# Two fp4 stages of a macaron block: the normalisation plan of group 2 is moved, and the last 64 features of the down product become two rounded-float32 products

## The chip, the cores and the metric

The kernel runs on one core of one Trainium2 chip. The metric is the device time in microseconds of one launch, weights' preparation included. A core has five engines with a queue each, worked in order: PE (matrix products), DVE (vector), ACT (activations), POOL (a second, slower vector engine) and SP (which issues transfers). They meet through semaphores only.

## The reference, cut to what matters

Six residual steps are applied to x of shape (8, 1024, 256). The first and the third are the fp4 feed-forward that the change touches:

```
def fp4_quant_dequant(x):                 # blocks of 16 along the last axis
    scale = max(max(abs(xb)) / 6, 1e-12)
    q = GRID[searchsorted(MID, abs(xb / scale))] * sign(xb) * scale
def fp4_linear(x, w):
    return einsum('bsk,nk->bsn', fp4_quant_dequant(x), fp4_quant_dequant(w))
h = silu(fp4_linear(x, w_gate)) * fp4_linear(x, w_up)      # 704 features
return fp4_linear(h, w_down)                               # back to 256
x = x + 0.5 * ffn(layernorm(x))
```

The others are a decayed linear attention, a ternary feed-forward (twice) and an attention with memories. Results are compared in float32.

## The kernel before, in words

x stays on the chip: 16 groups of 4 tiles, a tile being 128 tokens by 256. The stages follow one another: fp4, decay attention, fp4, ternary, memory attention, ternary. The function `ffn_fp4` is called twice, first with `prepare` set (it then also rounds and turns the down weights, and prepares later stages' weights).

One step i of its loop works on several tiles at once. PE multiplies tile i by gate and up in two halves of 352 (lines 835: `pg`, then `pu`), turns the scales of tile i-1 (line 863, once per step), and multiplies tile i-4 by the down weights: six 128x128 by 128x256 float32 products (line 932), the last of which holds 64 real features and 64 zeros. ACT applies silu to `pg` (line 846), DVE multiplies it by `pu` (line 848). DVE finds the block maxima of h (783 to 787), POOL divides by them (791), ACT makes the magnitudes (795) and in the next step DVE rounds in two passes (858), the second writing the grid values in bfloat16 to `gd`. SP turns `gd` by a transposing DMA into `gt` (884) and spreads the turned scales to a wide tile `ht` through DRAM (871, 876). Two steps later POOL multiplies `ht` by `gt` (899), and the step after it the tile goes into line 932. DVE adds the result to x (941).

Beside that, x of a coming group is normalised by ACT (317, 325, two tiles at a time) into the one buffer `xn`, divided by its scales (line 791 with `xn`), rounded in place by DVE (`mgx`, 858) and turned by a second transposing DMA, `gtx<-xn` (line 1048), which POOL multiplies with scales (899 with `xt`). For a group t this lies in steps 4t-7 (normalise tiles 0, 1), 4t-6 (scale), 4t-5 (normalise tiles 2, 3; round half 0), 4t-4 (scale half 1; DMA of half 0), 4t-3 (round half 1; POOL's product of half 0). The statistics come from a plan (`PLANS`, `statistics`, `advance`): sizes of batches and the step at which each is due; the shares of a batch are spread over the steps before it, and those due at step 0 (`first`) are worked off in the stage before by `begin`.

Every instruction of these stages is pinned behind the one pinned before it on its engine (`pin`), so the order in the queue is the order in the text; within a step of the loop: products with silu, copies of scales and magnitudes, `spread`, the DMA `gtx`, `advance`, normalising, POOL's products (`scaled_turn`), `scale` of h, x's scale and rounding, the down products. The last two tiles are turned on PE by `turn` (line 920) and not by DMA.

Of the kernel before, what the change touches and what calls it, by code (L numbers as in the profile page):

```python
# [9 lines left out]
F32 = mybir.dt.float32  # L10
F32R = mybir.dt.float32r
# [7 lines left out]
P = 128  # L19
D = 256  # L20
# [19 lines left out]
def macaron_kernel(  # L40
# [227 lines left out]
    def statistics(sizes, dues):  # L268
# [78 lines left out]
        "start": ((2, 1, 1, 2, 4, 4, 2), [max(0, G * (g - 2) + 1) for g in range(NG)]),  # L347
        "fp4": ((2, 1, 1, 2, 4, 4, 2), [max(0, G * (g - 2) + 1) for g in range(NG)]),
# [95 lines left out]
    wd = w_f0.tile([P, NC, D], F32, name="wd")  # L444
    nc.gpsimd.memset(wd[DCH[-1][1] :, NC - 1, :], 0.0)
# [190 lines left out]
    def prep_down_turn(ps, tag):  # L636
        for i, (k0, kn) in enumerate(DCH):
            pt = ps.tile([P, D], F32, tag=tag, name="ptd")
            for c in range(2):
                pin(  # L640
                    nc.tensor.transpose(
                        pt[:kn, c * P : (c + 1) * P], wd_n[:, c, k0 : k0 + kn], ident
                    )
                )
            pin(nc.scalar.copy(wd[:kn, i, :], pt[:kn, :]))
# [99 lines left out]
    def ffn_fp4(prepare, after):  # L745
        with ExitStack() as st:
# [13 lines left out]
            nc.gpsimd.memset(gd[:, NI:], 0.0)  # L760
# [18 lines left out]
            def scale(v, pool, at, mul=nc.gpsimd, sc=None):  # L779
# [10 lines left out]
                copies.append(lambda: pin(nc.scalar.copy(sc, sp)))  # L790
# [75 lines left out]
            def spread(i, pt):  # L866
# [19 lines left out]

                turn_grid()
# [16 lines left out]

            def scaled_turn(i):
                hs.pop(i)
                ht = spreading.pop(i)
                multiplied(ht, turning.pop(i))
                hts[i] = (ht, P)

            def turn(i):
                h, _ = hs.pop(i)
                ht = hp.tile([P, NC, P], F32, tag="ht", name="ht", bufs=HT_BUFS)
                for c0, c1 in ((0, 4), (4, 5), (5, 6)):
                    kn = DCH[c0][1]
                    pa = ps_t.tile([P, 4, P], F32, tag="pt", name="pt")
                    for c in range(c0, c1):
                        k0 = DCH[c][0]
                        pin(
                            nc.tensor.transpose(pa[:kn, c - c0, :], h[:, k0 : k0 + kn], ident)  # L920
                        )
                    pin(nc.scalar.copy(ht[:kn, c0:c1, :], pa[:kn, : c1 - c0, :]))
                hts[i] = (ht, DCH[-1][1])

            def down(i, ps=ps_o, tag="po"):
                g, j = divmod(i, G)
                ht, tail = hts.pop(i)
                po = ps.tile([P, D], F32, tag=tag, name="po")
                for c in range(NC):
                    kn = tail if c == NC - 1 else P  # L930
                    pin(
                        nc.tensor.matmul(  # L932
                            po,
                            lhsT=ht[:kn, c, :],
                            rhs=wd[:kn, c, :],
                            start=(c == 0),
                            stop=(c == NC - 1),
# [49 lines left out]

            xn = None
# [5 lines left out]
            for i in range(NT + 3):  # L994
                g, j = divmod(i, G)
                h = hp.tile([P, NI], F32, tag="h", name="h") if i < NT else None

                to = (i + 7) // G
                to_do = to < NG and i > 0
                half = 0 if j in (1, 2, 3) else 1  # L1000
# [43 lines left out]
                for to_, half_ in list(xgrids):  # L1044
                    gx, at = xgrids[to_, half_]
                    if at == i - 1:
                        gt = lnp.tile([P, G, P], BF16, tag="gtx", name="gtx", bufs=1)
                        pin(nc.sync.dma_start_transpose(out=gt, in_=gx))
                        xgrids[to_, half_] = (gt, at)
# [7 lines left out]
                if to_do and j % 2 == 1:  # L1057
                    if j == 1:
                        to_n, tiles = to, (0, 1)
                        if xn is None:  # L1060
                            xn = xn_pool.tile([P, G, D], F32, tag="xn", name="xn")
                    else:
                        to_n, tiles = (i + 5) // G, (2, 3)
                    if to_n < NG:
                        for n in tiles:
                            ln.normalize(xn, to_n, n, pin)
                if by_dma(i - 3):
                    scaled_turn(i - 3)
                if NT - 2 <= i - 2 < NT:
                    turn(i - 2)  # L1070
                for key in list(xgrids):
                    gt, at = xgrids[key]
                    if at == i - 2:
                        xgrids.pop(key)
                        to_m, half_m = key
                        multiplied(xts[to_m][:, G * half_m : G * half_m + G, :], gt)
                if i < NT:
                    own = scales[i % 2] if by_dma(i) else None
                    if own is not None:
                        scale(h, hp, NI, sc=own[:, : NI // 16])  # L1080
# [4 lines left out]
                    if j % 2 == 0 and i > 1:  # L1085
                        to_s, half_s = ((i + 6) // G, 0) if j == 2 else ((i + 4) // G, 1)
                        if 1 < to_s < NG:
                            scale(
                                x_part(half_s), lnp, NI + 88,
                                sc=own[:, NC * 8 : NC * 8 + 2 * D // 16],  # L1090
                            )
                            xhalf[i] = (to_s, half_s)
                    if j % 2 == 1 and i > 1:
                        to_r, half_r = ((i + 5) // G, 0) if j == 3 else ((i + 3) // G, 1)
                        if 1 < to_r < NG:
                            v = x_part(half_r)
# [988 lines left out]
```

## Time and profile before

| | us |
|---|---|
| three runs | 2606.8, 2608.18, 2610.64 |
| median | 2608.18 |
| the profiled execution | 2604.35 |
| its span in the profile | 2602.6 |
| fp4 stage 1, first gate product to last down product | 35 to 563 |
| fp4 stage 2, the same | 1006 to 1503 |
| busy over the span: PE, DVE, ACT, POOL | 2504, 2108, 1236, 903 |

The profile is one execution. Its parts used here are busy time by engine, busy shares in 40 slices, groups of instructions (busy time, mean of one, idle time before), the chain of work that ended last, and the timeline of instructions with the idle time before each and what ended it. L932 means line 932 of the kernel before.

### The profile page before, as it was taken

The page shows a single profiled execution, that of the slowest core. Times are in us where ns is not written, and L with a number is a line of the kernel's source. Part 1 is how long each engine was busy: PE and PEld are TensorE (multiplying, and loading weights), DVE is VectorE, ACT ScalarE, POOL GpSimd, SP SyncE. Part 2 cuts the span into 40 slices and gives each one's busy share as a digit, 9 for nine tenths or more (in the row PEclk, how much of TensorE's full clock was granted, in tenths as well). Part 3 has the DMA queues.
Part 4 walks back from the last instruction along what each step waited for, and adds up shares of the span by engine and source line. Part 5 has one row for each costly group of instructions (what it writes and reads, how often), then busy time and mean ns, then how long its engine had stood idle before and what let it go on. Part 6 is the DMA issues. An engine that isn't in the chain of part 4 may idle for free.

```text
span 2602.6 us, 52695 instructions
## 1 busy us (share of the span) xinstructions
PE 2504.2 (96%) x20426; PEld 1864.2 (72%) x20426; DVE 2107.9 (81%) x5040; ACT 1235.8 (47%) x2785; POOL 902.6 (35%) x895
## 2 busy tenths in 40 slices
PE   4899999999999998999999999999999999999999
PEld 2566776766666665677777789995677767678998
DVE  7899999858777678998889789657888888879864
ACT  5344444433433333444444366665555555437664
POOL 4555555521100102555555400004555555540000
PEclk9899999999999999999999999999999999999999
DMA  7455565510000001556555300000000000000001
GB/s 218 99 111 120 119 114 112 110 32 2 2 2 2 2 2 29 113 117 116 115 114 118 81 1 1 1 1 1 2 2 2 2 2 2 2 2 25 33 33 42
DMA packets 197883, 130.32 MB, mean 50 GB/s; under 512 B 137824, under 2 KB 173696, under 8 KB 197632
## 3 DMA queue, kind: packets, MB, share of 16 engines
q1 hardware_dynamic: 196688, 125.75, 22.3%
q8 instruction: 161, 2.64, 0.4%
q0 software_dynamic: 240, 0.54, 0.1%
q14 instruction: 90, 0.74, 0.1%
q10 hardware_dynamic: 704, 0.66, 0.1%
HBM read 78.67 MB, written 16.52 MB: 37 GB/s over the span
## 4 chain that ended last, share of the span: by engine, by line
PE 80%; DVE 11%; ACT 3%; DMA 3%; issue 2%; POOL 1%; SPq 1%; DVEq 0%; POOLq 0%; ACTq 0%
PE po L932 10%; PE po L1207 9%; PE pg L835 9%; PE ph L1180 9%; PE pu L835 8%; PE sc L1250 5%; PE py L1334 5%; PE pq L1348 4%; PE pkv L1348 4%; PE pk L1348 4%; PE po L1348 4%; PE py L1316 2%; PE pmo L1765 2%; DVE at L1259 1%; DMA gtx<-xn 1%
## 5 line engine op out<-in xcount | busy, mean ns | idle before, releaser
L835 PE MATMUL pg<-wgu,xt 128*128 128x352 f32 x1024 | 350.0, 465 | 13.4 <-ACT sg L846 13.1
L932 PE MATMUL po<-wd,ht 128*128 128x256 f32 x1536 | 356.0, 382 | 2.3 <-DVE x L941 1.8
L835 PE MATMUL pu<-wgu,xt 128*128 128x352 f32 x1024 | 348.9, 464 | 2.1 <-DVE h L848 1.9
L932 PEld LDWEIGHTS po<-wd,ht 128*128 128x128 f32 x1536 | 291.7, 191 | 66.0 <-issue 4.1
L791 POOL TENSOR_TENSOR h<-h,q_rs 128x704 f32<-128x704 f32 (+1 forms) x128 | 176.3, 1378 | 419.9 <-DVE q_rs L787 419.9
L846 ACT ACTIVATE sg<-pg 128x352 f32<-128x352 f32 x256 | 117.8, 460 | 399.3 <-PE pg L835 394.0
L835 PEld LDWEIGHTS pg<-wgu,xt 128*128 128x128 f32 x1024 | 194.9, 192 | 108.5 <-ACT sg L846 21.1
L835 PEld LDWEIGHTS pu<-wgu,xt 128*128 128x128 f32 x1024 | 187.1, 193 | 103.3 <-issue 14.7
L1207 PE MATMUL po<-w,hl 128*128 128x256 f32 x1024 | 243.9, 280 | 1.4 <-DVE hl L1191 1.2
L1207 PE MATMUL po<-w,hh 128*128 128x256 f32 x1024 | 243.4, 280 | 0.0
L1881 POOL TENSOR_TENSOR mo<-mo 128x256 f32<-128x256 f32 x192 | 164.3, 856 | 195.0 <-DVE mo L1778 186.5
L899 POOL TENSOR_TENSOR ht<-gt,ht 128x768 f32<-128x768 bf16 x124 | 206.4, 1664 | 0.0
L1180 PE MATMUL ph<-xh,w 128*128 128x512 f32 x512 | 204.4, 401 | 1.4 <-ACT hf L1188 0.6
L1180 PE MATMUL ph<-xl,w 128*128 128x512 f32 x512 | 202.2, 396 | 0.0
L1191 DVE TENSOR_TENSOR hl<-hf,hh 128x512 fp32r<-128x512 f32 x256 | 168.2, 683 | 39.6 <-ACT hh L1189 36.1
L1207 PEld LDWEIGHTS po<-w,hl 128*128 128x128 f32 x1024 | 192.1, 188 | 4.5 <-DVE hl L1191 2.5
L1207 PEld LDWEIGHTS po<-w,hh 128*128 128x128 f32 x1024 | 192.0, 188 | 2.6 <-DVE x L1215 0.3
L848 DVE TENSOR_TENSOR h<-sg,pu 128x352 f32<-128x352 f32 x256 | 131.6, 514 | 60.0 <-PE pu L835 53.1
L1188 ACT ACTIVATE hf<-ph,b1c 128x512 f32<-128x512 f32 x256 | 168.3, 696 | 18.5 <-PE ph L1180 16.1
L1259 DVE TENSOR_TENSOR at<-sc,dec 128x512 f32<-128x512 f32 x256 | 158.5, 681 | 16.6 <-PE sc L1250 16.5
L1259 DVE TENSOR_TENSOR at<-sc,tri 128x512 f32<-128x512 f32 x256 | 164.6, 678 | 0.4 <-PE sc L1250 0.4
L1189 ACT CAST hh<-hf 128x512 fp32r<-128x512 f32 x256 | 149.2, 628 | 17.0 <-PE po L1207 15.2
(276 smaller groups left out, 5304.0 us busy)
## 6 DMA issues: line engine op xcount, KB each, us to landing
ht<-sd SPq DMA_DIRECT2D x124, 384.0 KB
xt<-sd SPq DMA_DIRECT2D x56, 256.0 KB
sd<-sct SPq DMA_DIRECT2D x124, 64.0 KB
x<-in_x SPq DMA_DIRECT2D x15, 512.0 KB
out<-x SPq DMA_DIRECT2D x15, 512.0 KB
raw_w<-in_w_t SPq DMA_DIRECT2D x2, 1024.0 KB
gt<-gd SPq DMA_TRANSPOSE x124
gtx<-xn SPq DMA_TRANSPOSE x56
```

Source lines behind the costliest of these rows:

```text
L791: pin(mul.tensor_tensor(vb, vb, rs[:, :, None].to_broadcast([P, nb, 16]), ALU.mult))
L835: nc.tensor.matmul(ps, lhsT=xts[g][:, 2 * j + k, :], rhs=wgu[:, k, (2 * q + of_up) * NHALF : (2 * q + of_up + 1) * NHALF], start=(k == 0), ...
L899: nc.gpsimd.tensor_tensor(wide.rearrange("p c t -> p (c t)"), grid.rearrange("p c t -> p (c t)"), wide.rearrange("p c t -> p (c t)"), ALU. ...
L932: nc.tensor.matmul(po, lhsT=ht[:kn, c, :], rhs=wd[:kn, c, :], start=(c == 0), stop=(c == NC - 1),)
L1180: nc.tensor.matmul(ph, lhsT=w1[:, k, f * P : (f + 1) * P], rhs=xt[:, k, :], start=(k == 0 and xt is xh), stop=(k == 1 and xt is xl),)
L1188: nc.scalar.activation(hf, ph, AF.Gelu, bias=b1c[:, f : f + 1])
L1189: nc.scalar.copy(hh[:, f, :], hf)
L1191: nc.vector.tensor_tensor(hl[:, f, :], hf, hh[:, f, :].bitcast(F32), ALU.subtract)
L1207: nc.tensor.matmul(po, lhsT=ht[:, f, j * P : (j + 1) * P], rhs=w2[:, f, :], start=(f == 0 and ht is hh), stop=(f == NF - 1 and ht is hl),)
L1259: nc.vector.tensor_tensor(at, sc.rearrange("p m (e t) -> p (m e) t", e=2), weight, ALU.mult)
L1348: nc.tensor.matmul(dst, lhsT=lhsT, rhs=rhs, start=n == 0, stop=n == len(parts) - 1)
L1881: summed = nc.gpsimd.tensor_tensor(mo[:, :, :, 0, :], mo[:, :, :, 0, :], mo[:, :, :, m, :], ALU.add)
```

## The change

- The plan of stage 1 has group 2's statistics due one step later; in stage 2 the first batch is three groups, so that group 2's statistics are done ahead of the stage. In both stages group 2 is normalised in step 2 (tiles 0, 1; it was step 1) and step 3 (tiles 2, 3, as before), scaled in 3 and 4 (2 and 4), rounded in 4 and 5 (3 and 5). Later groups keep their steps.
- Within a step, POOL's products (`scaled_turn` and x's) now stand ahead of the issue of the DMA `gtx`, which stands ahead of normalising.
- The last 64 features are kept twice: ACT copies the last 64 columns of `gd` into the columns after them, and the last four scales likewise. The wide product of the last chunk thus holds them in 128 rows. `split` makes its rounded float32 `hh` (ACT) and the rest `hl` (POOL). The weights `ws` hold the rounded weights in 64 rows and the rest in the other 64. The sixth float32 product becomes `hh` by `ws` and `hl` by `ws`.
- The weights' preparation and `turn` make the doubled columns with POOL copies. Three memsets of zeros go.

```
-        "fp4": ((2, 1, 1, 2, 4, 4, 2), [max(0, G * (g - 2) + 1) for g in range(NG)]),
+        "start": ((2, 1, 1, 2, 4, 4, 2), [max(0, G * (g - 2) + 1 + (g == 2)) for g in range(NG)]),
+        "fp4": ((3, 1, 2, 4, 4, 2), [0 if g < 3 else G * (g - 2) + 1 for g in range(NG)]),
...
     def prep_down_turn(ps, tag, pool):
+        for c in range(2):
+            pin(nc.gpsimd.tensor_copy(wt[:, c], wd_n[:, c, None, NI - NK :].to_broadcast([P, 2, NK])))
...
+                pin(nc.scalar.copy(wh, pt))
+                pin(nc.scalar.copy(ws[:NK], pt[:NK]))
+                pin(nc.vector.tensor_tensor(ws[NK:], pt[NK:], wh[NK:].bitcast(F32), ALU.subtract))
...
-                copies.append(lambda: pin(nc.scalar.copy(sc, sp)))
+                copies.append(lambda: pin(nc.scalar.copy(sc[:, :nb], sp)))
+                if tail:
+                    copies.append(lambda: pin(nc.scalar.copy(sc[:, nb : nb + tail], sp[:, nb - tail :])))
...
+                pin(nc.scalar.copy(gd[:, NI:], gd[:, NI - NK : NI]))
                 turn_grid()
...
+            def split(ht):
+                hh = hp.tile([P, P], F32R, tag="hh", name="hh", bufs=3 if prepare else 2)
+                pin(nc.scalar.copy(hh, ht[:, NC - 1, :]))
+                hl = hp.tile([P, P], F32R, tag="hl", name="hl", bufs=3 if prepare else 2)
+                pin(nc.gpsimd.tensor_tensor(hl, ht[:, NC - 1, :], hh.bitcast(F32), ALU.subtract))
+                return hh, hl
             def scaled_turn(i):
                 multiplied(ht, turning.pop(i))
-                hts[i] = (ht, P)
+                hts[i] = (ht, *split(ht))
             def turn(i):
+                hd = lnp.tile([P, G, D], F32, tag="xn1", name="hd", bufs=1)[:, 0, 0:P]
+                pin(nc.gpsimd.tensor_copy(hd[:, 0:NK], h[:, NI - NK :]))
+                pin(nc.gpsimd.tensor_copy(hd[:, NK:], h[:, NI - NK :]))
...
             def down(i, ps=ps_o, tag="po"):
+                factors = [(ht[:, c, :], wd[:, c, :]) for c in range(NC - 1)]
+                factors += [(hh, ws), (hl, ws)]
...
+            for t in range(2, NG):
+                n01, s0, n23, r0, s1, r1 = (2, 3, 3, 4, 4, 5)
+                if t > 2:
+                    n01, s0, n23, r0, s1, r1 = (G * t + k for k in (-7, -6, -5, -5, -4, -3))
```

## The prediction, made before the change was run

> **What bounds the kernel now.** I read the page first: busy time, the slices, then the chain that ended last.
>
> ```profile
> PE 2504.2 (96%) x20426; PEld 1864.2 (72%) x20426; DVE 2107.9 (81%) x5040; ACT 1235.8 (47%) x2785; POOL 902.6 (35%) x895
> PE   4899999999999998999999999999999999999999
> DVE  7899999858777678998889789657888888879864
> PE 80%; DVE 11%; ACT 3%; DMA 3%; issue 2%; POOL 1%; SPq 1%; DVEq 0%; POOLq 0%; ACTq 0%
> ```
>
> PE sets the end, but DVE is above 0.8 in both fp4 stages (slices 1 to 8, 16 to 22). Busy time by stretch, a part of stage 1 and a part of stage 2 (PE, PEld, DVE, ACT, POOL):
>
> ```profile
> 130.00:260.00 130.00, 124.00 (x476) 86.96 (x475) 121.55 (x275) 53.24 (x134) 71.55 (x62) 1.00 0.58 115
> 1200.00:1400.00 200.00, 200.00 (x782) 144.82 (x781) 175.52 (x387) 86.84 (x218) 111.43 (x82) 1.00 0.57 115
> ```
>
> In stage 1 DVE is 93% busy and PE waits; in stage 2 from step 18 on PE never does. The chain in order of time, stage 2 and then the ternary stage, has the two prices that the change trades:
>
> ```profile
> 1194.19 2.59 PE po L932 x12
> ...
> 1571.65 7.54 PE po L1207 x64
> ```
>
> A float32 product is two PE instructions of 2.59/12 = 0.216 us; a rounded one of the same shape is one of 7.54/64 = 0.118. One step of stage 2, in the timeline:
>
> ```profile
> 1304.70 0.89 DVE L858 SCALAR_TENSOR_TENSOR gd<-qp,h 128x704 bf16<-128x704 f32 x1
> 1304.96 0.52 ACT L317 ACTIVATE xn<-x,ln_b 128x256 f32<-128x256 f32 x1
> 1305.82 0.52 DVE L848 TENSOR_TENSOR h<-sg,pu 128x352 f32<-128x352 f32 x1 [0.23 <-PE pu L835]
> 1306.87 0.58 ACT L795 ACTIVATE mgx<-xn 128x512 f32<-128x512 f32 x1
> 1308.13 1.35 DVE L858 SCALAR_TENSOR_TENSOR xn<-mgx,xn 128x512 f32<-128x512 f32 x2
> ```
>
> I call the second L848 of a step T (here 1305.82). ACT normalises before T here, and its `mgx` ends 0.7 us before DVE wants it. Then the fill and a transposing DMA of x, and the end of stage 1:
>
> ```profile
> 1024.90 2.71 PE L835 MATMUL pg<-wgu,xt 128*128 128x352 f32 x4 [4.66 <-ACT sg L846]
> ...
> 1062.73 1.20 SPq L1048 DMA_TRANSPOSE gtx<-xn  x1
> ...
> 1067.43 0.51 ACT L317 ACTIVATE xn<-x,ln_b 128x256 f32<-128x256 f32 x1 [1.63 <-DMA gtx<-xn]
> ```
> ```profile
> 545.87 0.47 ACT L795 ACTIVATE mg<-h 128x352 f32<-128x352 f32 x1
> 546.27 1.94 POOL L899 TENSOR_TENSOR ht<-gt,ht 128x768 f32<-128x768 bf16 x1
> 548.26 7.13 PE L932 MATMUL po<-wd,ht 128*128 128x256 f32 x24 [0.20 <-POOL ht L899]
> ```
>
> The first shows a PE stall of 4.66 us and then four products in 2.71 instead of 1.35: the granted clock fell (0.95 over 985 to 1060, 1.00 after). The next two: normalising overwrites the buffer that `gtx` reads, so ACT waits until the DMA, 4.7 us after issue, has landed.
>
> **The change, part by part.** Steps are counted by the scales' transpose (L863), one per step. With PE unhindered a step is 7.435 us.
>
> *Rounded products.* Per tile 2 x 0.216 - 2 x 0.118 = 0.196 us less PE, 25.1 over 128 tiles. Bounds: the page's group L1207 has 243.9 us busy for 1024, 0.238 each, overlap between its two groups counted; at that, a tile costs 2 x 0.238 - 0.432 = 0.04 more. I take 0.118, the pace on the chain. It reaches the end only where PE sets the step. From T to T the loop is DVE maxima, POOL, ACT, DVE rounding: where T runs late its length shows. Stage 2, steps 10 to 16 (two statistics tiles a step): 7.72 and 7.11 in turn, mean 7.42, no room under 7.24. Later catch-up steps take 6.6 to 6.9, so there is room. Stage 1: steps 8 to 35 and 43 to 52 average 7.7 to 7.8 with T late nearly throughout (ternary preparation), no gain; steps 35 to 43 and 52 to 58 run at 7.435. Gain: 44 steps of stage 2 and 14 of stage 1, 58 x 0.196 = -11.4.
>
> The Trainium skill ("TensorE: Matmul & The Clock Gate", Part 3, measured speedup) lets a weight load overlap a product in flight only if it loads other rows, and its LDWEIGHTS formula gives 107 ns for 128 columns. By that a pair would cost about 2 x 0.22 us (an estimate from that page) and the gain would vanish, 11.4 us worse. The ternary row, whose loads use all rows, is at 0.118, and decides here.
>
> *ACT's copy of `gd` and cast `hh`, every step.* The copy must wait for the second L858, which ends at T; before, ACT ran past it. Each is about 0.25 (a 128x128 copy, L869, takes 0.26). Behind them queue normalising (1.9) and `mgx` (0.58), so in odd steps `mgx` ends about T + 2.9 and DVE wants it at T + 2.31: up to 0.6 where none was lost, 0.3 where the DMA already held it. Silu of the next step, wanted at T + 3.5, is still free. Where PE has room this is hidden by it; where the loop sets the step it adds. 23 such odd steps at 0 to 0.6; I take 0.2, since the rows near it lose 0.3 and some touch PE's pace: +4.6. `hl` (POOL, about 0.4 by 1.06 for 512 and 1.93 for 1024 columns) ends near T + 0.9, before POOL is wanted at T + 2.5; the scales' extra copy (0.1) ends before L863 needs it (1.5 of room). Both nothing; without cover each adds its length per step.
>
> *Start of stage 2.* Gone from steps 0 and 1: four statistics (2.1) and the root's iterations (2.2), and normalising ahead of silu; the 4.66 stall and its slow clock go. The walk, each queue in its order with the rows' durations: DVE's statistics now end at 1016.65 (one left), its first gated product of step 1 at 1017.1 (was 1018.7), rounding at 1018.8; ACT's copy of `gd` ends at 1019.05 and silu of step 2 at 1019.5 (was 1024.8); h's maxima are done at 1020.4 and L863 of step 2 runs at 1021.0 instead of 1027.41. Step 3: ACT's copy (1025.4) and normalising (1027.3) hold silu, L863 waits for the copies of group 1's turned tile, 1031.2 instead of 1035.91. Step 4: 1036.4 instead of 1040.82. Step 5: DVE has both group 2's second scaling (1.45) and its first rounding (1.27), 1043.8 instead of 1048.66; T is 1047.8. Then step 5: half 0 is rounded in step 4, its DMA is issued in step 5, and group 3 is normalised into the same half in step 5. SP issues `gt` (now behind ACT's copy), `ht`, `xt`, then `gtx`, 2.7 us after `gt`; with 4.8 to land ACT stands until T + 7.6, then 1.9 + 0.58 before silu of step 6, which came at T + 3.5. That is `gt` at 1048.1, `gtx` at 1050.8, landed at 1055.6, silu at 1058.1 where it was at 1055.06: 3 late. PE's second `pg` of step 6 waits for it from 1050.4, 8 us, and starts cold; DVE's rounding waits for `mgx` meanwhile, so T of step 6 is 1063.6 instead of 1060.56. Sum +3; below it lies -5, if ACT needn't wait, above it +5.5, if the cold clock (2 x 1.25 on the row above) also reaches T. The DMA's issue also waits on the single `gtx` buffer in step 6, hidden by SP's gap. The statistics now lie in the decay stage (DVE 71% busy at its end): 0, at worst 2.1.
>
> *Start of stage 1.* The same iterations only move to step 2, and behind them normalising; what step 2 gains, step 3 returns, and step 4 gets both roundings: T about 1.4 late in step 5. There ACT's copies of the down weights (90.33) stand behind the DMA, landing near 95.9, + 1.9 + 0.58: 98.4, 8 late; PE needs them for its next work. A seventh copy and the DVE subtraction +0.5; POOL's doubling of the weights (two copies by 0.4) is done by then; two downs -0.4; about 1 for slack that the walk can't see. +7, between +1 without the wait and +9.
>
> *Ends of the stages.* `hh` of tile 60 waits for L899 (until 548.2), and the last tile's `mg` (545.87) queues behind it: 2.7 late. So are its rounding, POOL's L802 (550.95) and product for tile 61 (552.6), then `hh` on ACT and `hl` (553.35), then the two doubling copies (0.3 each by POOL's slope), which `turn` needs on PE before any down product: about 554.2 instead of 548.26. Four downs take back 0.8. Bounds 0 (all absorbed) and 6; +5 here. Stage 2's end has the same order: 1489.89 becomes about 1495.9, PE cold besides: +5.5.
>
> Sum: -11.4 + 4.6 + 3 + 7 + 5 + 5.5 = +13.7. The profiled execution took 2604.35 (span 2602.6), 3.8 under the median of the runs; the difference is put on the median: 2608.2 + 13.7 = 2622. 0.2%, 5.2 us, is about what a measurement can tell from no change.
>
> **Rivals.**
> - PE paces every step (not slower): the loop takes the extra ACT work inside 7.24. For it: PE 96%. Against it: stage 1's 7.7. -25.1 + 20.5 gives 2604; decides where the loop's mean is under 7.24.
> - ACT doesn't stand in step 5 (the transfer lands in time or the wait is elsewhere). Starts become -5 and +1: 2608. Against it: L317 is shown waiting on `gtx`.
> - Both: 2590.
> - Rounded products at 0.238: no 11.4, and 58 x 0.04 more: 2636.
>
> **How the numbers follow.** Mine 0.55 (own range 2611 to 2634), first rival 0.12, second 0.12, both 0.13, last 0.08. Low 2599 leaves out the both-case, 2636 holds the last. Faster: 0.13 and half the first, 0.19; same: the rest of the first, most of the second, a little of mine, 0.18; slower 0.63.
>
> **What would show it.** L1207-like pace 0.118 on the new products; stage 2 steps at 7.24; ACT idle about 7 us in step 5 before L317, released by `gtx`, in both stages, PE cold after it; no 4.66 stall in step 2; PE idle near 6 us before the last downs. Wrong if stage 1 steps shrink, or ACT's waits are short.

## The result, and the profile after

The changed kernel takes 2628.9 us (median of 6 runs, 2626.6 to 2631.6) against 2608.2 for the kernel before (6 runs, 2606.3 to 2610.6): a ratio of 1.0079, 95% interval 1.0066 to 1.0092. It is 20.7 us slower. Its profiled execution took 2628.72 us with a span of 2626.8; that of before 2604.35 with 2602.6, so the two profiles differ by 24.2 us, 3.5 more than the medians. In the changed kernel the down product is line 971, the gate and up products 860, ACT's second copy of `gd` 912, the cast `hh` 934, the difference `hl` 937, VectorE's rounding 883.

The page of the changed kernel, busy times, two of the slices and the chain:

```profile
PE 2490.1 (95%) x20426; PEld 1849.4 (70%) x20426; DVE 2105.6 (80%) x5029; ACT 1294.9 (49%) x3158; POOL 958.7 (36%) x1030
PE   4799999989999999899999899999999999999999
DVE  8799898848777678898989779756888888889864
PE 72%; DVE 14%; ACT 5%; DMA 3%; issue 3%; POOL 1%; SPq 0%; ACTq 0%; DVEq 0%; POOLq 0%
```

PE does 14.1 us less work (2504.2 before), and the kernel is longer all the same: its share of the chain that ended last fell from 80% to 72%, and DVE's rose from 11% to 14%. The two stretches shown of before, in the same columns (window, length, then PE, PEld, DVE, ACT and POOL busy):

```profile
130.00:260.00 130.00, 120.86 (x469) 82.50 (x468) 119.32 (x270) 57.68 (x176) 77.64 (x76) 1.00 0.53 110
1200.00:1400.00 200.00, 199.84 (x803) 144.63 (x802) 179.36 (x398) 101.08 (x303) 124.77 (x111) 1.00 0.60 118
```

In stage 1 PE waits more than before. In stage 2 it is full as it was, and does more instructions in the same 200 us (803 for 782). One step there, in the timeline of PE:

```profile
1303.13 2.32 PE L971 MATMUL po<-wd,ht 128*128 128x256 f32 x10
1305.10 0.47 PE L971 MATMUL po<-ws,hh 128*128 128x256 f32 x1
1305.40 0.28 PE L971 MATMUL po<-ws,hl 128*128 128x256 f32 x1
...
1310.37 2.32 PE L971 MATMUL po<-wd,ht 128*128 128x256 f32 x10
```

The next tile's product starts 7.24 us after this one; before it was 7.435. The 0.196 us are there, wherever PE sets the pace.

Where the rest went is read from the scales' transposition (one per step): the times between such marks split both spans in the same places. The stretch from the 7th to the 59th mark is called the middle of a stage below.

| stretch (us) | before | after | difference |
|---|---|---|---|
| up to the first mark of stage 1 | 45.98 | 43.95 | -2.0 |
| stage 1, 1st to 7th mark | 64.68 | 72.37 | +7.7 |
| stage 1, 7th to 59th | 400.09 | 404.07 | +4.0 |
| from there to stage 2's first mark | 504.44 | 509.93 | +5.5 |
| stage 2, 1st to 7th mark | 49.66 | 54.72 | +5.1 |
| stage 2, 7th to 59th | 388.10 | 384.25 | -3.9 |
| from there to the end | 1149.65 | 1157.51 | +7.9 |

Only one stretch of steps gained (the first mark lies at 44.0 to 47.2 us over all the kernels here, so the -2.0 tells nothing), and by less than half of the 10.2 us that 0.196 us a step would give its 52 steps. The starts: stage 2, step 2, and then step 5 on ACT, SP's queue and PE:

```profile
1034.64 1.45 PE L860 MATMUL pg<-wgu,xt 128*128 128x352 f32 x4 [0.47 <-ACT sg L871]
...
1065.57 1.21 SPq L1102 DMA_TRANSPOSE gtx<-xn  x1
...
1071.91 0.51 ACT L317 ACTIVATE xn<-x,ln_b 128x256 f32<-128x256 f32 x1 [8.88 <-DMA gtx<-xn]
...
1074.82 2.72 PE L860 MATMUL pg<-wgu,xt 128*128 128x352 f32 x4 [9.28 <-ACT sg L871]
```

The stall of 4.66 us is 0.47 now. In its place ACT stands 8.88 us for `gtx`, PE 9.28, and the four products after it take 2.72 us where warm ones take 1.35; the granted clock over them was 0.50. The Trainium skill ("TensorE: Matmul & The Clock Gate", Part 1, "What's actually happening") says that the array goes back to half clock after an idle window of about 3.4 us; this row agrees, and the last section shows falls behind shorter gaps. Stage 1 has the same wait:

```profile
93.32 0.51 ACT L317 ACTIVATE xn<-x,ln_b 128x256 f32<-128x256 f32 x1 [8.46 <-DMA gtx<-xn]
...
96.15 0.69 PE L655 MATMUL ptd<-ident,wd_n 128*128 128x128 f32 x2 [12.84 <-ACT wd L657]
```

A step that the loop of ACT, POOL and VectorE sets (stage 2, step 11, which takes 8.29 us), on DVE and ACT:

```profile
1118.54 0.89 DVE L883 SCALAR_TENSOR_TENSOR gd<-qp,h 128x704 bf16<-128x704 f32 x1
...
1119.46 0.24 ACT L912 COPY gd<-gd 128x64 bf16<-128x64 bf16 x1 [2.65 <-DVE gd L883]
...
1121.70 0.58 ACT L820 ACTIVATE mgx<-xn 128x512 f32<-128x512 f32 x1
...
1122.37 1.42 DVE L883 SCALAR_TENSOR_TENSOR xn<-mgx,xn 128x512 f32<-128x512 f32 x2 [0.64 <-ACT mgx L820]
```

ACT is idle for 2.65 us in front of its copy, since the grid isn't rounded yet; the normalising and `mgx` behind it come late, and DVE, which had no such wait in the step shown of before, stands 0.64 us. Last, the end of stage 2:

```profile
1506.28 0.30 ACT L934 CAST hh<-ht 128x128 fp32r<-128x128 f32 x1 [6.51 <-POOL ht L925]
...
1511.71 0.24 POOL L954 COPY hd<-h 128x64 f32<-128x64 f32 x1
...
1512.00 0.48 PE L959 MATMUL pt<-ident,hd 128*128 128x128 f32 x1 [6.83 <-POOL hd L954]
1512.27 3.77 PE L971 MATMUL po<-wd,ht 128*128 128x256 f32 x10
```

PE stands 6.83 us for POOL's copy, which is the last of a line: POOL's product, ACT's cast, the magnitudes behind the cast, the last tile's rounding, another product, cast and difference, then the copies.

### The profile page after: what moved, and what is told of

Its sections match the earlier page's. It is cut to its first block, busy times and chain, and to the rows that moved or that the text cites. A ratio compares the mean times of both kernels' runs of the same rounds, so it can differ in the third digit from the quotient of the medians.

```text
span 2626.8 us, 53163 instructions
## 1 busy us (share of the span) xinstructions
PE 2490.1 (95%) x20426; PEld 1849.4 (70%) x20426; DVE 2105.6 (80%) x5029; ACT 1294.9 (49%) x3158; POOL 958.7 (36%) x1030
## 4 chain that ended last, share of the span: by engine, by line
PE 72%; DVE 14%; ACT 5%; DMA 3%; issue 3%; POOL 1%; SPq 0%; ACTq 0%; DVEq 0%; POOLq 0%
PE po L1238 9%; PE ph L1211 9%; PE po L971 7%; PE pg L860 7%; PE pu L860 6%; PE sc L1281 5%; PE py L1365 4%; PE pq L1379 4%; PE pk L1379 4%; PE pkv L1379 4%; PE po L1379 4%; PE py L1347 2%; DMA gtx<-xn 2%; PE pmo L1796 2%; DVE at L1290 1%
## 5 line engine op out<-in xcount | busy, mean ns | idle before, releaser
L971 PE MATMUL po<-wd,ht 128*128 128x256 f32 x1280 | 304.1, 386 | 2.5 <-DVE x L976 2.5
L971 PEld LDWEIGHTS po<-wd,ht 128*128 128x128 f32 x1280 | 245.8, 194 | 59.5 <-POOL xn L816 5.7
L860 PEld LDWEIGHTS pg<-wgu,xt 128*128 128x128 f32 x1024 | 183.4, 191 | 131.0 <-ACT sg L871 56.4
L860 PEld LDWEIGHTS pu<-wgu,xt 128*128 128x128 f32 x1024 | 187.7, 193 | 100.0 <-issue 10.5
L1501 POOL TENSOR_TENSOR x<-x,ob 128x1024 f32<-128x1024 f32 x16 | 37.7, 2356 | 335.0 <-ACT xn L317 335.0
```

The costliest lines, as they stand in the source:

```text
L860: nc.tensor.matmul(ps, lhsT=xts[g][:, 2 * j + k, :], rhs=wgu[:, k, (2 * q + of_up) * NHALF : (2 * q + of_up + 1) * NHALF], start=(k == 0), ...
L971: nc.tensor.matmul(po, lhsT=left, rhs=right, start=(n == 0), stop=(n == NC))
```

## The experiments

Two accounts were set against each other. The first is the prediction's: several separate costs, each at its place (ACT's wait in step 5, ACT's copy and cast in the loop-limited steps, a queue at the ends), that add up. The rivals put the loss on one part: on the split everywhere, or on the new steps of the third group.

Each ratio is to runs of the kernel before taken beside the run (medians 2606.8 to 2608.2).

| run | us | ratio to before (95%) |
|---|---|---|
| split alone | 2645.3 | 1.0141 (1.0124 to 1.0158) |
| schedule alone | 2620.0 | 1.0044 (1.0029 to 1.0058) |
| before, three groups' statistics ahead | 2602.4 | 0.9978 (0.9969 to 0.9987) |
| changed, fourth group normalised in step 6 | 2611.4 | 1.0012 (1.0002 to 1.0021) |
| split alone, cast ahead of normalising | 2616.0 | 1.0024 (1.0013 to 1.0035) |
| step 6 + copy by VectorE | 2610.0 | 1.0011 (1.0001 to 1.0022) |
| step 6 + last four tiles in float32 | 2598.6 | 0.9961 (0.9947 to 0.9976) |
| combination | 2599.8 | 0.9963 (0.9948 to 0.9978) |
| split in stage 2 alone, 64 rows in stage 1 | 2611.5 | 1.0016 (1.0007 to 1.0025) |
| step 6, no second copy | 2601.9 | 0.9983 (0.9974 to 0.9992) |
| step 6, split made and not used | 2625.6 | 1.0070 (1.0054 to 1.0085) |
| split for tiles 17 to 59 of stage 2 | 2595.5 | 0.9959 (0.9946 to 0.9973) |

A difference of two of these carries 3 to 6 us of uncertainty by the intervals; where less is claimed below, it is read from the profiles' marks.

### Split alone

```diff
-        "fp4": ((3, 1, 2, 4, 4, 2), [0 if g < 3 else G * (g - 2) + 1 for g in range(NG)]),
+        "fp4": ((2, 1, 1, 2, 4, 4, 2), [max(0, G * (g - 2) + 1) for g in range(NG)]),
...
-                n01, s0, n23, r0, s1, r1 = (2, 3, 3, 4, 4, 5)
+                n01, s0, n23, r0, s1, r1 = (1, 2, 3, 3, 4, 5)
...
```

Against the changed kernel; the plan "start" and the order of the parts within a step also go back to those of before.

> The split alone: the rounded products with their copies, cast and difference as in the changed kernel; the plans of the statistics, the steps in which the third group is normalised, scaled and rounded, and the order of the parts within a step are those of before. Theory of separate costs (the profile's differences, stage by stage: steady steps +4.0 in stage 1 and -3.9 in stage 2, end of stage 1 +5.2, end of stage 2 +7.6, starts +11.3): the starts' share is not paid, so about 2608.2 + 13 = 2621 us, between 2617 and 2625. Rival 1 (the split's copies on ACT cost the starts too, and the new steps nothing): 2629. Rival 2 (the new steps of the third group carry all of the loss, and the split breaks even): 2608.

Measured: 2645.3 us, 37 us slower than before and 16 slower than with the schedule. No theory had this. The starts are as cheap as expected (66.2 and 49.0 us from the 1st to the 7th mark, 64.7 and 49.7 before), but the steps after them take 415.6 and 400.0 us in the two stages, where the changed kernel has 404.1 and 384.3: nearly every second step of stage 2 is far over 7.24, most at 7.7 to 8.0, up to the end. ACT and POOL in such a step:

```profile
1305.62 0.24 ACT L910 COPY gd<-gd 128x64 bf16<-128x64 bf16 x1 [1.60 <-DVE gd L881]
...
1307.99 0.28 ACT L932 CAST hh<-ht 128x128 fp32r<-128x128 f32 x1
...
1311.31 0.76 ACT L818 ACTIVATE qp<-h 128x704 f32<-128x704 f32 x1 [2.01 <-POOL h L814]
```
```profile
1308.35 0.46 POOL L935 TENSOR_TENSOR hl<-ht,hh 128x128 fp32r<-128x128 f32 x1 [2.98 <-ACT hh L932]
1308.77 1.17 POOL L923 TENSOR_TENSOR xt<-gtx,xt 128x512 f32<-128x512 bf16 x1
1309.89 1.39 POOL L814 TENSOR_TENSOR h<-h,q_rs 128x704 f32<-128x704 f32 x1
```

The cast comes 2.4 us after the copy, since in the order of before four normalising instructions stand between them. POOL waits 2.98 us for it with `hl`, and behind `hl` stands the product that ACT's next magnitudes wait for. So the costs do not simply add: the changed kernel's order within a step is needed by the split, and that reading became a theory of its own (below).

### Schedule alone

```diff
-                factors = [(ht[:, c, :], wd[:, c, :]) for c in range(NC - 1)]
-                factors += [(hh, ws), (hl, ws)]
...
+                for c in range(NC):
+                    kn = tail if c == NC - 1 else P
...
```

Everything of the split goes back to the code of before; plans, steps and order stay as changed.

> The schedule alone: plans, steps of the third group and order within a step as in the changed kernel; the down product is that of before, in float32, with no copy of gd, no cast and no difference. Theory of separate costs: only the two starts are paid (+5.9 and +5.4 us in the profiles), so about 2608.2 + 11 = 2619 us, between 2615 and 2622, with ACT's wait of 8 to 9 us for gtx in step 5 of both stages. Rival 1 (all comes from the split): 2604, the gain of the statistics ahead alone. Rival 2 (all comes from the steps): 2629.

Measured: 2620.0, 11.8 us slower than before, as the first account had it. ACT waits in step 5 of both stages, here even longer, since neither copy nor cast stands ahead of it:

```profile
96.57 0.51 ACT L317 ACTIVATE xn<-x,ln_b 128x256 f32<-128x256 f32 x1 [13.54 <-DMA gtx<-xn]
1065.44 0.51 ACT L317 ACTIVATE xn<-x,ln_b 128x256 f32<-128x256 f32 x1 [11.02 <-DMA gtx<-xn]
```

### Three groups' statistics ahead, and nothing else

```diff
-        "fp4": ((2, 1, 1, 2, 4, 4, 2), [max(0, G * (g - 2) + 1) for g in range(NG)]),
+        "fp4": ((3, 1, 2, 4, 4, 2), [0 if g < 3 else G * (g - 2) + 1 for g in range(NG)]),
```

Against the kernel before.

> Before, with one line changed: the first share of the statistics ahead of the second stage has three groups in place of two; steps, order and the down product stay. Theory of separate costs: the 4.66 us for which PE stands in step 2 of stage 2 go, and nothing new is waited for in step 5, since the third group's tiles are rounded a step earlier than in the changed kernel: 4 to 6 us faster, 2602 to 2604 us. Rival (the statistics' time is only moved ahead of the stage, where PE waits for it all the same): 2608, within 1 us.

Measured: 2602.4, 5.8 us faster. From the 1st to the 7th mark stage 2 takes 44.6 us instead of 49.7, and in step 5 ACT waits for `gtx` 0.87 us, where the changed kernel waits 8.88:

```profile
1046.29 0.51 ACT L317 ACTIVATE xn<-x,ln_b 128x256 f32<-128x256 f32 x1 [0.87 <-DMA gtx<-xn]
```

From the 59th mark of stage 1 to the first of stage 2 it takes 504.2 us (before 504.4): the statistics themselves cost nothing ahead of the stage.

### The fourth group's tiles in step 6

```diff
+                if t == 3:
+                    n01 += 1
                 norms[n01, 0], norms[n23, 1] = t, t
```

> The changed kernel, with the fourth group's tiles 0 and 1 normalised in step 6 in place of step 5 in both stages, so that ACT does not stand in front of the transfer gtx of the third group; all else is kept. Theory of separate costs: the idle time of 8.5 to 9.3 us before L317 goes in both stages, and with it the cold clock after it (1.3 us); up to 1 us of it comes back in step 6, where the scale of these tiles now follows their normalising in the same step: 10 to 15 us faster than the changed kernel, 2614 to 2619 us. Rival (the wait only moves: what ACT does next stands for the same transfer, or the fourth group comes late for step 12): 2627 to 2630.

Measured: 2611.4, 17.5 us faster than the changed kernel and somewhat more than expected. The first seven marks take 66.0 and 45.2 us (72.4 and 54.7). Step 5 of stage 2 on ACT, and the products that start step 6 on PE:

```profile
1057.14 0.30 ACT L934 CAST hh<-ht 128x128 fp32r<-128x128 f32 x1
1057.34 0.59 ACT L820 ACTIVATE mgx<-xn 128x512 f32<-128x512 f32 x1
1058.80 0.47 ACT L871 ACTIVATE sg<-pg 128x352 f32<-128x352 f32 x1 [0.87 <-PE pg L860]
```
```profile
1059.78 1.35 PE L860 MATMUL pg<-wgu,xt 128*128 128x352 f32 x4
```

`mgx` follows the cast at once, and PE has neither wait nor slow clock. The steps after it lengthen (8.89 and 8.50 us for steps 6 and 7, 7.72 and 7.24 in the changed kernel), so 2.4 us come back there; the rest of the wait didn't move elsewhere, it went.

### Split alone, with the cast ahead of normalising

```diff
+                if by_dma(i - 3):
+                    scaled_turn(i - 3)
                 for half in range(2):
                     if (i, half) in norms:
...
-                if by_dma(i - 3):
-                    scaled_turn(i - 3)
```

Against the split alone; plans and steps are still those of before.

> The split with the plans and steps of before, as in the run of the split alone (2645.3 us), with one move: within a step the product of grid and scales, ACT's cast hh and POOL's difference hl of a down tile now stand ahead of the four normalising instructions on ACT, as in the changed kernel, and not behind them. Theory of the queue (from that run's trace: in every second step the cast starts 2.4 us late behind four normalisations, POOL stands 3 us for it, and the products of POOL that ACT's next magnitudes wait for come after; steps alternate 7.24 and 7.78 us to the end): the steps fall back to 7.24 us, some 20 of each stage by 0.5 us, so 20 to 26 us faster than the split alone, 2619 to 2625 us. Rival (the steps of the third group or the order of the transfers are what the split can't stand): 2640 to 2646.

Measured: 2616.0, 29 us faster than the split alone and 3 below the range of the theory. The middle of stage 2 takes 384.2 us (400.0), that of stage 1 403.5 (415.6), the values of the changed kernel. The same step on ACT and POOL:

```profile
1298.59 0.24 ACT L910 COPY gd<-gd 128x64 bf16<-128x64 bf16 x1 [0.55 <-DVE gd L881]
1298.74 0.29 ACT L932 CAST hh<-ht 128x128 fp32r<-128x128 f32 x1
1299.00 0.51 ACT L317 ACTIVATE xn<-x,ln_b 128x256 f32<-128x256 f32 x1
```
```profile
1299.11 0.46 POOL L935 TENSOR_TENSOR hl<-ht,hh 128x128 fp32r<-128x128 f32 x1 [1.02 <-ACT hh L932]
```

One move of two lines is worth more than the whole difference between the kernels before and after. The theory of the queue holds; that the steps of the third group or the transfers' order were to blame falls.

### The second copy made by VectorE

```diff
-                pin(nc.scalar.copy(gd[:, NI:], gd[:, NI - NK : NI]))
...
+                            pin(
+                                nc.vector.scalar_tensor_tensor(
+                                    gd[:, NI:], qp[:, NI - NK : NI], FP4_LEAST,
+                                    hs[i - 1][0][:, NI - NK :], ALU.max, ALU.subtract,
+                                )
+                            )
```

Against the kernel with step 6, as in the next run and in the two with `split made and not used` and `no second copy`.

> The changed kernel with the fourth group's normalising in step 6 (2611.4 us), and the second copy of the grid's last 64 features made by VectorE (the second rounding done once more on 64 columns) in place of ACT's copy, which stood in ACT's queue until VectorE had rounded. Theory (the copy in ACT's queue holds up ACT's next magnitudes in the steps that are limited by the loop of ACT, VectorE and POOL; steps 10 to 16 of stage 2 take 8.30 us where before took 7.44 to 7.72): these steps fall by 0.3 to 0.6 us, some 5 in stage 2 and 10 in stage 1, so 4 to 8 us faster, 2604 to 2607. Rival (VectorE is itself in that loop, and its 0.2 us more in every step cost what ACT's wait cost): 2610 to 2614.

Measured: 2610.0 against 2611.4, no difference that can be told. Steps 11, 13 and 15 of stage 2 do fall from 8.30 to 7.85 us, but steps late in the stage rise (8.5 to 9.2, 8.0 to 9.0). The rival's number came; which of VectorE's waits takes the gain back was not followed.

### The last four tiles in float32

```diff
-                hts[i] = (ht, *split(ht))
+                hts[i] = (ht, *split(ht)) if i < NT - 4 else (ht, None, None)
...
+                    if c1 == NC:
+                        pin(nc.tensor.transpose(pa[:, 3, :], h[:, NI - P :], ident))
...
+                if hh is None:
+                    factors += [(ht[:, NC - 1, :], ws.bitcast(F32))]
+                else:
+                    factors += [(hh, ws), (hl, ws)]
```

> The changed kernel with the fourth group's normalising in step 6 (2611.4 us), and the last four tiles of each stage without cast and difference: their last 64 features, held twice, are multiplied in float32 with the two parts of the weights, rounded and rest, which add up to the weights; the last two tiles get their second copy from one more transposition on TensorE in place of two copies on POOL. Theory (at the end of a stage the cast, the difference and POOL's copies stand in line one after the other, +5.5 us behind stage 1 and +4.7 behind stage 2 in this kernel against the run with the statistics ahead alone): 7 to 10 us faster, 2601 to 2605. Rival (the end is set by VectorE's rounding of the last tile, and the queue only fills the wait for it): 2609 to 2612.

Measured: 2598.6, 12.7 us faster than with step 6 alone, more than the theory's 7 to 10. The stretch behind the 59th mark of stage 1 falls from 510.1 to 504.2 us, that of stage 2 from 1157.6 to 1151.5, almost to the values of before (504.4, 1149.7). The end of stage 2 on PE:

```profile
1480.96 0.27 PE L959 MATMUL pt<-ident,h 128*128 128x128 f32 x1
1482.15 4.02 PE L978 MATMUL po<-wd,ht 128*128 128x256 f32 x10 [0.92 <-POOL ht L925]
1486.00 0.59 PE L978 MATMUL po<-ws,ht 128*128 128x256 f32 x2
```

The idle time of 6.83 us is 0.92. So the queue of cast, difference and copies set the end, not VectorE's rounding.

### The combination

It joins the third group's steps and the "start" plan of before with the changed kernel's order and "fp4" plan, VectorE's copy, and the last four tiles in float32.

> The split with the changed kernel's order within a step, the third group normalised, scaled and rounded in the steps of before (1, 2, 3, 4, 5), three groups' statistics ahead of the second stage and the plan of the first stage as before, VectorE's second copy of the grid's last features, and the last four tiles without cast and difference. Theory (costs and gains add: rounded products about 11 us off the steps that TensorE paces, statistics ahead 5.8 off, nothing at the ends, some loop-limited steps a little longer): 2588 to 2597 us. Rival (the split's costs in the loop-limited steps stay): 2600 to 2606.

Measured: 2599.8. It is 8.4 us faster than before, but the gains don't add: the time lies just below the rival's 2600 to 2606 and above the theory's 2597. The middle of stage 1 takes 403.0 us. With split and copy it is 401.8 to 404.8 in all kernels of the changed order, and three of these have the same code there (changed, step 6, last four tiles in float32: 404.1, 401.8, 404.8), so one execution can be off by 1.5 us; the kernels without split and copy, on 128 rows, have 400.1 to 401.7. The split gains nothing there.

### The split in the second stage alone

```diff
-                hts[i] = (ht, *split(ht))
+                hts[i] = (ht, *split(ht)) if i < (0 if prepare else NT - 4) else (ht, None, None)
...
+                if hh is None:
+                    factors += [(ht[:NK, NC - 1, :], wf[:NK])]
```

`wf` is a tile of its own with the 64 rows of the weights.

> Stage 1 with the down product of before (float32, no second copy, no cast, no difference), stage 2 with the split; its last four tiles, and all of stage 1, multiply their last 64 features in float32 by the weights themselves, kept in a tile of their own. Otherwise as in the combination: third group in the steps of before, three groups' statistics ahead of stage 2, the changed kernel's order within a step, VectorE's second copy. Theory (in stage 1 the split loses more in the loop-limited steps than it gains in the others: 403.0 to 404.8 us between the scales' transpositions of steps 6 and 58 against 400.1 to 401.4 without it; in stage 2 it gains, 382.2 against 388.1): stage 1 as in the run with the statistics ahead, first transposition of stage 2 at 1015.4 us, and behind it the 1577 us of the combination: a span of 2592.4, so 2592 to 2597 us. Rival (stage 1's share comes from the first loads and not from the split): 2599 to 2602.

Measured: 2611.5, which neither had. Stage 2 came as expected (44.9, 382.3 and 1151.5 us), but its first mark only at 1029.8: every step of stage 1 that PE paces takes 7.83 us, where before takes 7.44. The groups of PE from 300 to 450 us:

```profile
L975 PE MATMUL po<-wd,ht 128*128 128x256 f32 x190 | 44.2, 379 | 0.4 <-DVE x L980 0.4
L975 PE MATMUL po<-wf,ht 64*128 64x256 f32 x38 | 13.2, 428 | 0.0
```

and the weight loads around that product, in PE's timeline of loads:

```profile
305.82 0.29 PEld L975 LDWEIGHTS po<-wf,ht 64*128 64x128 f32 x2 [0.33 <-issue]
306.45 0.89 PEld L862 LDWEIGHTS pg<-wgu,xt 128*128 128x128 f32 x4 [0.33 <-issue]
```

The edit had changed one thing more than meant: the last product is on 64 rows, where before has 128 of which half are zero. Its own loads and those of the product behind it each come 0.33 us late. The last run tests this.

### Without the second copy

```diff
-                pin(nc.scalar.copy(gd[:, NI:], gd[:, NI - NK : NI]))
...
+            nc.gpsimd.memset(gd[:, NI:], 0.0)
```

> The changed kernel with the fourth group's normalising in step 6 (2611.4 us), without ACT's second copy of the grid's last 64 features: the second half of the doubled chunk is zero, so the weights' rest is left out of the product for these features; cast, difference and products stay. Theory (the copy stands in ACT's queue until VectorE's second rounding ends, and holds up the next magnitudes): pairs of loop-limited steps fall from 15.63 towards 15.1 us, some 4 pairs in stage 2 and 7 in stage 1, so 4 to 7 us faster, 2604 to 2607. Rival (in these steps the loop stands for POOL and for VectorE, not for ACT's copy, as moving the copy to VectorE gained only 1.3 us): 2609 to 2613.

Measured: 2601.9, 9.4 us faster by the medians and 7.6 by the ratios, where the theory had 4 to 7. In the profiles the middle of stage 2 is 3.9 us shorter and that of stage 1 2.6, together 6.5, which is within it. Steps 11, 13 and 15 of stage 2 fall from 8.30 to 7.6 and 7.7. Step 11, on ACT and DVE:

```profile
1095.05 0.51 ACT L317 ACTIVATE xn<-x,ln_b 128x256 f32<-128x256 f32 x1
...
1096.95 0.58 ACT L821 ACTIVATE mgx<-xn 128x512 f32<-128x512 f32 x1
```
```profile
1098.14 1.35 DVE L884 SCALAR_TENSOR_TENSOR xn<-mgx,xn 128x512 f32<-128x512 f32 x2
```

Without the copy ACT normalises while DVE still rounds (until 1095.92), and DVE finds `mgx` ready. That the copy's wait is what lengthens these steps is shown by this. The run also lets SP issue `gt` earlier, as the grid is complete without the copy; but VectorE's copy delays `gt` too, and with it these steps already fell by 0.45 of the 0.6 to 0.7. That a copy elsewhere is free is refuted by VectorE's.

### The split made, and not used

```diff
-                factors += [(hh, ws), (hl, ws)]
+                factors += [(ht[:, NC - 1, :], ws.bitcast(F32))]
```

> The changed kernel with the fourth group's normalising in step 6 (2611.4 us); second copies, casts and differences are all made, but the last product takes the doubled features in float32 times rounded weights and rest, in place of the two rounded products: two instructions at float32's pace instead of two at the rounded pace, and nothing else. Theory (in a step that PE paces, the rounded products are worth 0.196 us, and 34 of stage 1 and 45 of stage 2 run at 7.24): 79 times 0.196, less what the loop's slack takes up: 11 to 15 us slower, 2622 to 2627. Rival (the rounded products are not what shortens the steps): 2610 to 2614.

Measured: 2625.6, 14.2 us slower than the same kernel with the rounded products, as the theory had it. The steps that ran at 7.24 run at 7.44. Where the loop sets the pace nothing is lost: steps 10 and 11 of stage 2 take 15.62 us together, and 15.64 with the rounded products. In the profiles the middle of stage 1 is 3.1 us longer and that of stage 2 7.1. So the rounded products by themselves are worth 10.2 us in the middles of these two executions, and 14.2 by the medians, which carry the uncertainty above.

### The split where PE paces

```diff
+            def splits(i):
+                return not prepare and 17 <= i < NT - 4
...
+                if splits(i):
+                    pin(nc.scalar.copy(gd[:, NI:], gd[:, NI - NK : NI]))
...
+    nc.gpsimd.memset(wf[NK:], 0.0)
...
+                hts[i] = (ht, *split(ht)) if splits(i) else (ht, None, P)
...
+                    factors += [(ht[:hl, NC - 1, :], wf[:hl])]
```

`P` is the number of rows taken here (a tile that isn't split carries it in the place of `hl`).

> Stage 1 with the float32 product throughout, its last 64 features now as 128 rows, the lower 64 of features and weights zero, as in the kernel before; stage 2 with the split for tiles 17 to 59 alone, where TensorE paces the steps, and ACT's second copy for these tiles only; the other tiles in float32 on 128 rows. Plans and steps as in the run that split all of stage 2 (2611.5 us). Theory 1 (the last product on 64 rows in place of 128 is what made every step of stage 1 in that run 7.83 us and not 7.44): stage 1's steps return to 7.44, 10 to 14 us less. Theory 2 (the split pays where PE paces and nowhere else): first transposition of stage 2 at 1015.4 us as in the run with the statistics ahead, steps 1 to 6 at 44.6, then 388.1 less 42 times 0.196, and 1150 to 1152 behind step 58: a span of 2590 to 2592, so 2591 to 2596 us, the fastest of all. Rival to 1 (the weights' tile or the plan makes stage 1 slow): stage 1 stays at 7.83, 2603 or more. Rival to 2 (the split's first steps bring a new stall): 2597 to 2602.

Measured: 2595.5, the lowest of all medians: 0.9959 of before (0.9946 to 0.9973), not to be told from the 0.9961 and 0.9963 of the last four tiles in float32 and of the combination. The last two tiles of each stage, turned on PE, stay on 64 rows, as in the kernel before. Stage 1's steps are back at 7.44 us, and the same groups of PE from 300 to 450 us now read:

```profile
L980 PE MATMUL po<-wd,ht 128*128 128x256 f32 x200 | 46.5, 379 | 0.4 <-DVE x L985 0.4
L980 PE MATMUL po<-wf,ht 128*128 128x256 f32 x40 | 11.9, 379 | 0.0
```

So the 64 rows were the cost. The middle of stage 2 takes 380.7 us (388.1 before): 7.4 us, near 0.196 for each of the 38 steps among them that multiply tiles from 17 on, which run at 7.24; with the split for all of stage 2's tiles but the last four, and VectorE's copy, it took 382.2 and 382.3. The span of the profile, 2596.1, is 4 us above the expected one: the first mark of stage 2 came at 1017.3 instead of 1015.4, and the stretch behind step 59 took 1153.6.

## Why the prediction was right, and where it wasn't

2622 was predicted, with 2599 to 2636 around it; 2628.9 was measured. The sign and the mechanisms hold. In the profiles the difference is 24.2 us, 10.5 more than the +13.7 of the sum: 6.9 of these in the steps (-6.8 predicted, +0.1 measured in the two middles), 2.9 at the ends, 2.1 at the start of stage 2, and -1.3 at the start of stage 1 counted from the start of the span.

- **Rounded products, -11.4.** The pace of 0.118 held, against the rival with 0.238 and the skill's rule that was weighed there (it stands in Part 3 of that page under "The mechanism"). Undoing them alone costs 14.2 us by the medians; in the profiles it costs 3.1 and 7.1 us in the two middles, where the prediction had 2.7 (14 steps) and 8.6 (44). Some 79 steps of the kernel with step 6 run at 7.24, more than the 58 counted, but by the marks the loop-limited steps between them take most of that gain back in stage 1, and the prediction's count, only of steps where the loop isn't behind, came nearer; the medians don't decide between 11.4 and the 15.5 of 79 steps.
- **ACT's copy and cast, +4.6.** This is the mis-sized term. The copy alone costs 9.4 us by the medians and 6.5 in the two middles of the profiles (the run without it), 0.28 to 0.41 for each of the 23 odd steps instead of 0.2. The step named the mechanism, `mgx` up to 0.6 us late because the copy waits for VectorE's second rounding; in step 11 DVE's wait is 0.64, and steps 11, 13 and 15 of stage 2 lose 0.6 to 0.7 each by the copy, so there the far end of that bound was the better choice. Together with the products, the two middles should have gained 6.8 us by the prediction; they gained nothing (+4.0 and -3.9, or -2.9 in sum between the kernel with step 6 and the run with the statistics ahead). Products and copy give -3.7 of it; what the cast, the scales' copy and the new order cost in the steps was not measured one by one.
- **`hl` on POOL, nothing.** In the changed order POOL waits for the cast (2.38 us at 1304 and 1.01 at 1311) and, with `hl` done, stands again before its next work (1.41 and 0.51 us), so `hl` holds nothing up there; no run takes it out by itself. The prediction read the cast's place in ACT's queue without seeing that this place is what keeps `hl` free: behind the normalising it costs 29 us.
- **Start of stage 2, +3.** The gain ahead of step 5 was right: 4.9 predicted (1043.8 instead of 1048.66), 5.0 measured between the 1st and the 5th mark, and 5.1 between the 1st and the 7th in the run with the statistics alone. Steps 5 and 6 cost 10.0 more than before, where the prediction had 7.9. The wait was 8.88 us on ACT and 9.28 on PE, predicted about 7 and 8; moving it away gives back 9.6 between the same marks. The net is +5.1, near the bound of 5.5 that was set for a cold clock reaching VectorE's loop; how much of the excess the clock made was not separated, since the transfer also took longer (6.3 us from its issue to ACT's start, 4.7 in the row that was used).
- **Start of stage 1, +7.** +7.7 between the marks, +5.7 counted from the start of the span. Right, with a part of it (1 for slack that the walk can't see) a guess.
- **Ends, +5 and +5.5.** +5.5 and +7.9. The order of the queue and its length were right: from the last mark to the last run of down products it is 14.6 us in both stages before and 20.4 after, 5.8 more (5.9 and 6.0 predicted), and taking the queue away gave 5.9 and 6.1 us back. The second was too small: PE stood 6.83 us and then ran ten products in 3.77 us instead of 2.32.
- **Rivals.** PE does not pace every step (the middle of stage 1 grew). ACT does stand in step 5; the kernel in which it doesn't is the run with step 6: its starts come to +1.3 and -4.5 against before (this rival had +1 and -5), and its 2611.4 is near the 2608 that the rival gave. Both together, 2590, is what no kernel here reached.

The terms measured one at a time are -14.2 + 9.4 for the steps, +11.8 for the schedule and +12.7 for the ends: +19.7, near the 20.7 of the whole. Each of them carries 3 to 6 us of uncertainty, so that the sum comes so close is partly luck. All but the schedule were taken on the kernel with step 6, and the split alone (+37) and the combination show that such a sum holds only as long as the order in the queues does.

## What to carry to other kernels

A cheap instruction costs what its place in an in-order queue makes it cost: before adding one that waits, look at what stands behind it, and put the instruction that another engine waits for ahead of the long work. Apply a change that saves time on one engine only to the steps which that engine paces; in the others it brings its side work and no gain. And before a buffer is reused one step earlier, look for the transfer that still reads it.

## What the runs showed of the hardware that wasn't expected

A product on 64 rows between products on 128 rows costs more than the same product on 128 rows with half of them zero: 7.83 us a step against 7.44, 0.39 us more, with 0.33 us in front of its own weight loads and of those behind it. The Trainium skill ("TensorEngine Tiling (Array Packing)", "Key Properties") says that a change of the tiling mode drains the array; two changes a step with a gap at each are what one would then see, though no run here tells a drain from another cause of the gap.

The same short gaps cost the clock in one execution and not in another. In the run with the last four tiles in float32, PE stood only 1.57 and 0.92 us before the last products of stage 2, with a few transpositions between, and ten products took 4.02 us all the same. The combination has the same gaps at the same place, and there the ten took 2.42. Busy times by stretch for the two ends, in this order (window, length, then PE, PEld, DVE, ACT and POOL busy, the granted clock, the transfers' share and GB/s):

```profile
1478.40:1482.15 3.75, 1.26 (x11) 0.82 (x9) 3.54 (x10) 2.25 (x8) 3.34 (x3) 0.98 0.00 0
1482.15:1486.20 4.05, 4.05 (x11) 3.34 (x12) 2.62 (x3) 0.03 (x1) 2.31 (x2) 0.60 0.00 2
1478.10:1481.90 3.80, 1.37 (x10) 0.93 (x8) 3.59 (x10) 2.19 (x8) 3.28 (x3) 1.00 0.00 0
1481.90:1484.30 2.40, 2.34 (x11) 2.08 (x12) 2.33 (x3) 0.09 (x1) 2.37 (x3) 1.00 0.00 0
```

In the first the clock stays at 0.98 through the gaps and falls to 0.60 over the products behind them, as it was 0.62 behind the stall of 6.83 us in the changed kernel; in the second it stays at 1.00. The kernel before does both by itself: PE stands 1.37, 0.63 and 0.20 us at either end, and its 24 products behind that took 7.13 us at the end of stage 1 (granted clock 0.76) but at the end of stage 2 (1.00):

```profile
1489.89 5.45 PE L932 MATMUL po<-wd,ht 128*128 128x256 f32 x24 [0.20 <-POOL ht L899]
```

So neither the longest gap nor the busy share before the products (1.26 of 3.75 us and 1.37 of 3.80) tells whether the clock falls, and what does is not shown here. An end that is 1.5 us longer or shorter may be no more than this.
